# PSUM shared out anew in a four-layer graph kernel: three tiles for pairs, one for sums, one for rows

## The chip, the cores and the metric

The kernel runs on one core of a Trainium2 chip. A core has a matrix engine (TensorE, PE in the profile), a vector engine (VectorE, DVE), a scalar engine (ScalarE, ACT), a general engine (GpSimd, POOL) and a queue for DMA (SyncE, SP). Each engine works through its own queue of instructions in order and waits at semaphores for the others. The metric is the device time of one execution in microseconds (us), taken as the median of several runs. A profile shows one execution, with the start, the duration and the cause of waiting of every instruction.

## The reference

There are N = 4096 nodes with D = 64 features, and a dense 0/1 adjacency matrix `adj` of 4096x4096 float32 (64 MB). Four layers follow one another, each with a residual and a layer norm:

```python
x = _layernorm(x + _L0_gnn_ref(x, adj, L0_gnn_W, L0_gnn_b), axis=-1)
x = _layernorm(x + _L1_gnn_ref(x, adj, L1_gnn_r, L1_gnn_w_att, L1_gnn_b_att), axis=-1)
x = _layernorm(x + _L2_gnn_ref(x, adj, L2_gnn_weight, L2_gnn_bias), axis=-1)
x = _layernorm(x + _L3_gnn_ref(x, adj, L3_gnn_att_w, L3_gnn_att_b), axis=-1)
```

Layer 0 takes the mean over the neighbours, a linear map, a relu and a division by the norm. Layers 1 and 3 are hyperbolic attention: for every pair (i, j) of nodes the weight is `sigmoid(left_i + right_j) * adj_ij`, it multiplies the logarithmic map from x_i to x_j, and the sum over j is mapped back (`expmap`, `proj`). Layer 2 gives the last neighbours of each row the weights 1, 1/2, 1/4 and so on (by a count of the neighbours) and adds up a linear map of x with them.

## The kernel before, in words

The function `stream` (L569) computes everything on one core. Rows of the result are taken in 4 groups of 1024 (`GROUPS`, 3, 2, 1, 0). The nodes that are summed over come in 32 blocks of 128, taken in 16 pairs from the last to the first. Each layer reads `adj` once: a pair of blocks for one group is an edge tile of 128x2x1024 float32, 1 MB, loaded by SP's queue into a ring of six (`loads`). A program for inputs that don't fit this form stands behind it and isn't executed here.

**Attention** (`attention`, `attend`, `move`). For each block of a pair, six matmuls on PE put the pair values of 128 nodes with 1024 rows into a PSUM tile z of 128x1024 (L945, L948, L951, two halves of 512 each). ACT computes a sigmoid `sig` (L953) and a square `sq` of z (L956), DVE multiplies (L959, `t`). After both blocks DVE makes one more product over the pair (L961), and PE adds `t` up into the PSUM tile `acc` by four matmuls (L965). At the end of a group ACT copies `acc` to `sums` (L972). `move` (L982) then does the closing work of a group: some 75 small DVE operations on 128x8 (among them three reciprocal roots by Newton steps, L673 to L679), with the rows of `u_1` copied by ACT in two parts (L1002) out of a matmul (L1000), ACT's L1008 and L1034, POOL's L1007 and L1081, and DVE's L1085 as its end. `u_1` has one buffer. `linear` (L1088) prepares the next layer's supports, `prepare` (L791) and `spread_left` (L906) the rows and columns for the next attention.

**Layer 2.** For each block `count` (L1382) adds to a running count in a z tile by matmuls with two fixed matrices (`pass_by`, `enter`, L1386), ACT makes the weights by an exp (`weights_of`, L1395), and `add_up` (L1398, matmuls at L1401) multiplies them with the supports. `wide_pass` (L1323) treats groups 3 and 2 in turn within each block, two chains of counts; `narrow_pass` (L1353) then treats groups 1 and 0 one after another, by halves of 512 rows. `check` (L751) is a large DVE operation that tests the adjacency values, on one half of the edge tiles in layer 0 and the other half in layer 2.

**What sets the order.** Small work of the groups lies in two queues of generators; `tick(n)` lets them advance by n steps at fixed places of the main loops, `need` makes them run on until a part is done. In layers 0 and 2 the order of PE and ACT is that of the program text (`tc.manual_schedule` with `FIXED`); DVE's order there, and every engine's in layers 1 and 3, is set by the scheduler of the programming layer, from dependencies and its own estimates.

**PSUM.** There are eight banks of 128x512 float32. Before, z has two tiles of two banks, `acc` two of one bank, and `aux`, the tile for all small row work (`take`, `free`, `held`: the generators use it one after another), two of one bank.

Where group sums of layer 0 end, `end_0` (L1191) takes both `aux` tiles, one for each half of the group.

Of the kernel before, what the change touches and what calls it, by code (L numbers as in the profile page):

```python
# [10 lines left out]
F32 = mybir.dt.float32  # L11
# [10 lines left out]
D = 64  # L22
# [36 lines left out]
def gnn_stack_kernel(  # L59
# [509 lines left out]
    def stream(fits):  # L569

        with ExitStack() as st:
# [9 lines left out]
            aux = pool("f_aux", 2, space=PSUM)  # L581
# [323 lines left out]

            def spread_left(s):  # L906

                left_bs[s] = lefts.tile([P, WW], F32, name="left_b")
                for h in range(2):
                    yield from free()  # L910
                    t = take(F32, P, W)
                    for k in range(SB):
                        nb = s * WB + h * SB + k
                        nc.tensor.transpose(
                            t[:, k * P : (k + 1) * P],
                            left[:, nb : nb + 1].to_broadcast([P, P]),
                            ident,
                        )
                    yield near()
                    nc.scalar.copy(left_bs[s][:, h * W : (h + 1) * W], t)  # L920
                    held.pop()
                    yield 1

            def attend(layer, s, rate, then):
# [3 lines left out]
                acc = ps.tile([P, W], F32, name="acc")  # L928
                for g in reversed(range(NB // 2)):
# [4 lines left out]
                    sq = sb.tile([P, 2, WW], F32, name="sq")  # L934
                    t = sb.tile([P, 2, WW], F32, name="t")
                    for k in (1, 0):
# [3 lines left out]
                        zp = ps.tile([P, WW], F32, name="z")  # L940
                        for h in range(2):
                            half = zp[:, h * W : (h + 1) * W]
                            to = slice(s * WW + h * W, s * WW + (h + 1) * W)
                            at = k * WW + h * W
                            nc.tensor.matmul(  # L945
                                half, two_i, edge[:, at : at + W], start=True, stop=False
                            )
                            nc.tensor.matmul(  # L948
                                half, hi_lo[:, of], lo_hi[:, to], start=False, stop=False
                            )  # L950
                            nc.tensor.matmul(half, src[:, of], dst[:, to], start=False, stop=True)  # L951
                        sig = sb.tile([P, WW], F32, name="sig")
# [188 lines left out]
            with ExitStack() as lp:  # L1141
# [49 lines left out]
                def end_0(s, tops):  # L1191
                    z = grp("z0")
                    ts = []
                    yield from free()
                    for top, low in tops:
                        t = take(F32, P, SB, P)
                        for k in range(SB):
                            cols = slice(k * P, (k + 1) * P)
                            to = t[:, k, : D + 1]
                            nc.tensor.matmul(to, top[:, cols], sum_w, start=True, stop=False)  # L1200
                            nc.tensor.matmul(to, low[:, cols], count_w, start=False, stop=True)
                        ts.append(t)
                    for h, t in enumerate(ts):
# [74 lines left out]
            ps = pool("p_ps", 2, space=PSUM)  # L1278
# [44 lines left out]
            def wide_pass(two):  # L1323

                zs = [ps.tile([P, WW], F32, name="z") for _ in two]

                accs = [None, None]
                behind, lag = [None, None], []
                for g in reversed(range(NB // 2)):
                    edges = [load_2(s, g) for s in two]  # L1330
                    need((2, 2 * g // WB))
                    for k in (1, 0):
                        j = 2 * g + k
                        for i, edge in enumerate(edges):
# [15 lines left out]
                lag.pop(0)()  # L1350
                return accs

            def narrow_pass(s):  # L1353

                zs = [ps.tile([P, WW], F32, name="z") for _ in range(2)]
# [35 lines left out]
            def weights_of(z, n, w=None):  # L1391

                if w is None:
                    w = sb.tile([P, 2, WW], F32, name="sq").bitcast(BF16)[:, 0, :n]
                nc.scalar.activation(w, z[:, :n], AF.Exp, bias=at_edge, scale=-LN2)  # L1395
                return w
# [113 lines left out]
```

## Time and profile before

| quantity | before |
|---|---|
| median of 3 runs | 1141.41 us (1140.45 to 1144.33) |
| profiled execution, its own time | 1140.81 us |
| its span, first to last instruction | 1139.1 us |
| mean granted clock of PE | 0.972 |
| layer 0, until the first L959 | 0 to 190.8 us |
| layer 1, first L959 to the end of the last L961 | 190.8 to 532.3 us |
| layer 2, wide pass, then narrow passes | about 529 to 640, then to 775 us |
| layer 3, first L959 to the end of the last L961 | 775.7 to 1109.6 us |
| last L961 to the end | 29.5 us |

In the profile an engine's share is its busy time over the span. A line of the groups gives the operation, its output and inputs, its count, the busy time in us, the mean in ns, and the idle time just before it with what ended most of it. A line of the timeline gives the start, the duration, the instruction, and in brackets the idle time before it and its releaser. PEld is PE's loading of weights, which runs beside its matmuls. The stages overlap at their borders: the first counts of layer 2 start before the last product of layer 1 ends.

### The profile page before, as it was taken

The page shows a single profiled execution, that of the slowest core. Times are in us where ns is not written, and L with a number is a line of the kernel's source. Part 1 is how long each engine was busy: PE and PEld are TensorE (multiplying, and loading weights), DVE is VectorE, ACT ScalarE, POOL GpSimd, SP SyncE. Part 2 cuts the span into 40 slices and gives each one's busy share as a digit, 9 for nine tenths or more (in the row PEclk, how much of TensorE's full clock was granted, in tenths as well). Part 3 has the DMA queues.
Part 4 walks back from the last instruction along what each step waited for, and adds up shares of the span by engine and source line. Part 5 has one row for each costly group of instructions (what it writes and reads, how often), then busy time and mean ns, then how long its engine had stood idle before and what let it go on. Part 6 is the DMA issues. An engine that isn't in the chain of part 4 may idle for free.

```text
span 1139.1 us, 13626 instructions
## 1 busy us (share of the span) xinstructions
PE 1021.6 (90%) x4949; PEld 391.2 (34%) x4949; DVE 956.0 (84%) x1882; ACT 821.2 (72%) x894; POOL 66.1 (6%) x97
## 2 busy tenths in 40 slices
PE   6999897899999899998999997798899999998981
PEld 3545544233333333332333232232333333333320
DVE  6687898999999899999653476528999999999996
ACT  0003216899989789787766778888898998987970
POOL 0020120000000000100100020000000001001001
PEclk8999998999999999999999999899999999999995
DMA  8999998545666466564988976676455665665500
GB/s 342 422 391 405 373 415 337 196 166 203 215 206 219 154 209 221 180 204 154 322 305 301 341 263 233 233 257 231 164 206 188 218 222 194 222 221 183 196 0 23
DMA packets 38419, 271.58 MB, mean 238 GB/s; under 512 B 4550, under 2 KB 4550, under 8 KB 5574
## 3 DMA queue, kind: packets, MB, share of 16 engines
q1 hardware_dynamic: 37440, 269.50, 65.8%
q10 hardware_dynamic: 902, 1.12, 0.3%
q8 instruction: 41, 0.67, 0.2%
q14 instruction: 36, 0.29, 0.1%
HBM read 269.55 MB, written 1.05 MB: 238 GB/s over the span
## 4 chain that ended last, share of the span: by engine, by line
DVE 53%; PE 29%; ACT 8%; DMA 6%; POOL 2%; issue 2%; ACTq 0%; SPq 0%; POOLq 0%; DVEq 0%
DVE t L959 21%; DVE t L961 20%; PE z L1386 10%; DMA edges<-in_adj_dram 6%; PE acc L1401 5%; PE acc L1243 4%; PE acc L965 2%; ACT sig L953 2%; ACT sq L956 2%; ACT sq L1395 1%; PE aux L1106 1%; PE aux L852 1%; PE z L945 1%; DVE junk L751 1%; PE z L951 1%
## 5 line engine op out<-in xcount | busy, mean ns | idle before, releaser
L953 ACT ACTIVATE sig<-left_b,right 128x1024 f32<-128x1024 f32 x256 | 293.8, 1149 | 46.5 <-DVE t L959 36.5
L959 DVE SCALAR_TENSOR_TENSOR t<-z,sig 128x1024 f32<-128x1024 f32 x256 | 310.0, 1216 | 5.9 <-ACT sq L956 5.0
L956 ACT ACTIVATE sq<-z,turn 128x1024 f32<-128x1024 f32 x256 | 281.5, 1106 | 22.8 <-PE z L951 20.7
L961 DVE SCALAR_TENSOR_TENSOR t<-sq,t 128x2048 f32<-128x2048 f32 x128 | 292.9, 2288 | 0.7
L965 PE MATMUL acc<-t,xe 128*64 128x512 f32 x1024 | 255.2, 611 | 28.5 <-DVE t L961 24.4
L945 PE MATMUL z<-edges,two_i 128*128 128x512 bf16 x512 | 201.7, 394 | 21.5 <-DVE t L959 21.5
L951 PE MATMUL z<-dst,src 74*128 74x512 f16 x512 | 195.2, 381 | 0.0
L948 PE MATMUL z<-lo_hi,hi_lo 128*128 128x512 f16 x512 | 194.1, 379 | 0.0
L1395 ACT ACTIVATE sq<-z,at_edge 128x512 bf16<-128x512 f32 (+1 forms) x192 | 153.0, 830 | 53.3 <-PE z L1386 51.9
L965 PEld LDWEIGHTS acc<-t,xe 128*64 128x64 f32 x1024 | 63.6, 137 | 163.0 <-DVE t L961 85.9
L751 DVE SCALAR_TENSOR_TENSOR t<-edges 128x2048 bf16<-128x2048 f32 x32 | 74.0, 2312 | 44.2 <-DMA edges<-in_adj_dram 44.1
L1386 PE MATMUL z<-edges,pass_by 128*128 128x512 bf16 x248 | 89.6, 401 | 15.9 <-ACT sq L1395 15.8
L945 PEld LDWEIGHTS <-two_i 128*128 128x128 bf16 x512 | 50.2, 98 | 143.8 <-issue 96.6
L1243 PE MATMUL acc<-edges,first 128*128 128x512 bf16 x256 | 80.6, 396 | 20.0 <-DMA edges<-in_adj_dram 19.8
L1386 PE MATMUL z<-edges,enter 128*128 128x512 bf16 x256 | 90.8, 397 | 0.0
L1401 PE MATMUL acc<-sq,halves 128*64 128x512 bf16 x512 | 82.6, 401 | 3.6 <-ACT sq L1395 2.9
L1243 PE MATMUL acc<-edges,third 128*65 128x512 bf16 x256 | 80.5, 396 | 0.0
L751 DVE SCALAR_TENSOR_TENSOR junk<-edges 128x2048 bf16<-128x2048 f32 x32 | 73.1, 2285 | 4.7 <-DMA edges<-in_adj_dram 4.5
L948 PEld LDWEIGHTS <-hi_lo 128*128 128x128 f16 x512 | 50.3, 98 | 68.8 <-issue 25.5
L951 PEld LDWEIGHTS <-src 74*128 74x128 f16 x512 | 49.2, 96 | 67.5 <-issue 2.3
L1081 POOL TENSOR_TENSOR w_att<-x,p 128x512 f32<-128x512 f32 x8 | 12.9, 1615 | 495.0 <-DVE q L1079 495.0
L1243 PEld LDWEIGHTS <-first 128*128 128x128 bf16 x256 | 24.1, 98 | 48.9 <-issue 21.3
(262 smaller groups left out, 771.3 us busy)
## 6 DMA issues: line engine op xcount, KB each, us to landing
edges<-in_adj_dram SPq DMA_DIRECT2D x256, 1024.0 KB, 4.9
x<-in_x_dram SPq DMA_DIRECT2D x4, 256.0 KB
out_dram<-x ACTq DMA_DIRECT2D x4, 256.0 KB
w_sb<-in_L_gnn_W_dram ACTq DMA_DIRECT2D x1, 32.0 KB, 5.1
given<-in_L_gnn_b_dram ACTq DMA_DIRECT2D x1, 0.2 KB
given<-in_L_gnn_bias_dram ACTq DMA_DIRECT2D x1, 0.2 KB
given<-in_L_gnn_b_att_dram ACTq DMA_DIRECT2D x1, 0.0 KB
given<-in_L_gnn_att_b_dram ACTq DMA_DIRECT2D x1, 0.0 KB
```

Source lines behind the costliest of these rows:

```text
L751: V.scalar_tensor_tensor(junk, a, 0.0, a, ALU.not_equal, ALU.not_equal, accum_out=odd[:, n : n + 1])
L945: nc.tensor.matmul(half, two_i, edge[:, at : at + W], start=True, stop=False)
L948: nc.tensor.matmul(half, hi_lo[:, of], lo_hi[:, to], start=False, stop=False)
L951: nc.tensor.matmul(half, src[:, of], dst[:, to], start=False, stop=True)
L953: nc.scalar.activation(sig, left_b, AF.Sigmoid, bias=right[:, j : j + 1])
L956: nc.scalar.activation(sq[:, k], zp, AF.Square, bias=turn, scale=-1.0 / UNIT)
L959: V.scalar_tensor_tensor(t[:, k], zp, 0.0, sig, ALU.max, ALU.mult)
L961: V.scalar_tensor_tensor(t, sq, HIGH**2, t, ALU.add, ALU.mult)
L965: nc.tensor.matmul(acc[h * D : (h + 1) * D, :], xe[:, j, :], t[:, k, h * W : (h + 1) * W], start=j == BLOCKS[0], stop=j == BLOCKS[-1],)
L1243: nc.tensor.matmul(accs[h][:m], lhs[:, j, :], edge[:, at : at + W], start=j == BLOCKS[0], stop=j == BLOCKS[-1],)
L1386: nc.tensor.matmul(z[:, h : h + W], lhs, rhs[:, h : h + W], start=j == BLOCKS[0], stop=True, skip_group_check=True,)
L1395: nc.scalar.activation(w, z[:, :n], AF.Exp, bias=at_edge, scale=-LN2)
```

## The change

PSUM is shared out anew: z three tiles, `acc` one, `aux` one (3x2 + 1 + 1 banks). In attention the sums of a pair are issued two pairs later: after the z matmuls of the first block of pair g, those of pair g + 2 are added up, with an ordering edge (`in_order`) that keeps them behind these matmuls in the scheduler's order; the last two pairs of a group follow at its end. `sig` gets three buffers instead of two; `sq` and `t` are allocated after these matmuls. `end_0` takes its two halves one after another through the single `aux`. In the wide pass of layer 2, the counts of both chains stand side by side, then the sums of both, one block late: c c w w instead of c w c w. Both accumulators lie in one z tile, and one `sq` tile holds the weights of both chains. The narrow pass is only renamed.

```diff
-            aux = pool("f_aux", 2, space=PSUM)
+            aux = pool("f_aux", 1, space=PSUM)
...
+            def in_order(one, behind):
+
+                tc.add_manual_dep(
+                    one, behind.name,
+                    mybir.DependencyInfo(
+                        mybir.DependencyClass.NoSync, mybir.DependencyReason.DATA
+                    ),
+                    reason="order of issue",
+                )
...
+                lag = []
+
+                def add_up(g, t, behind=None):
+
+                    for k in (1, 0):
+                        j = 2 * g + k
+                        for h in range(2):
+                            it = nc.tensor.matmul(
+                                acc[h * D : (h + 1) * D, :], xe[:, j, :],
+                                t[:, k, h * W : (h + 1) * W],
+                                start=j == BLOCKS[0], stop=j == BLOCKS[-1],
+                            )
+                            if behind is not None:
+                                in_order(it.ins, behind.ins)
+
...
-                    sq = sb.tile([P, 2, WW], F32, name="sq")
-                    t = sb.tile([P, 2, WW], F32, name="t")
...
-                        zp = ps.tile([P, WW], F32, name="z")
+                        zp = z_tile()
...
+                        if k == 1:
+                            if len(lag) == 2:
+                                add_up(*lag.pop(0), last)
+                            sq = sb.tile([P, 2, WW], F32, name="sq")
+                            t = sb.tile([P, 2, WW], F32, name="t")
+                        sig = sb.tile([P, WW], F32, name="sig", bufs=3)
...
-                    for k in (1, 0):
-                        j = 2 * g + k
-                        for h in range(2):
-                            nc.tensor.matmul(
-                                acc[h * D : (h + 1) * D, :], xe[:, j, :],
-                                t[:, k, h * W : (h + 1) * W],
-                                start=j == BLOCKS[0], stop=j == BLOCKS[-1],
-                            )
+                    lag.append((g, t))
                     tick(rate)
+                for args in lag:
+                    add_up(*args)
...
-                    ts = []
-                    yield from free()
-                    for top, low in tops:
+                    for h, (top, low) in enumerate(tops):
+                        yield from free()
                         t = take(F32, P, SB, P)
...
-                        ts.append(t)
-                    for h, t in enumerate(ts):
...
                         V.tensor_mul(zz, t[:, :, :D], over(d))
+                        held.pop()
                         V.tensor_add(zz, zz, xw[:, at, :])
-                    held.clear()
+                        if h == 0:
+                            yield near()
...
-            ps = pool("p_ps", 2, space=PSUM)
+            ps = pool("p_ps", 1, space=PSUM)
+
+            def z_tile():
+                return ps.tile([P, WW], F32, name="z", bufs=3)
...
-                zs = [ps.tile([P, WW], F32, name="z") for _ in two]
-
-                accs = [None, None]
+                zs = [z_tile() for _ in two]
+
+                both = z_tile()
+                accs = [both[:, :W], both[:, W:]]
...
+                        w = sb.tile([P, 2, WW], F32, name="sq").bitcast(BF16)[:, :, :WW]
                         for i, edge in enumerate(edges):
                             here = edge[:, k * WW : (k + 1) * WW]
                             count(zs[i], behind[i], here, j, WW)
                             behind[i] = here
-                            while lag:
-                                lag.pop(0)()
-                            w = weights_of(zs[i], WW)
-
-                            def add(i=i, j=j, w=w):
-                                if accs[i] is None:
-                                    accs[i] = ps.tile([P, W], F32, name="acc")
-                                add_up(accs[i], j, w[:, :W], w[:, W:])
-
-                            lag.append(add)
+                            weights_of(zs[i], WW, w[:, i])
+                            if i == 1:
+                                for of, acc in enumerate(accs if lag else ()):
+                                    add_up(acc, *lag[of])
+                                lag = [(j, w[:, n, :W], w[:, n, W:]) for n in range(2)]
...
-                lag.pop(0)()
+                for of, acc in enumerate(accs):
+                    add_up(acc, *lag[of])
```

More of the change, by code (lines that the diff above doesn't have):

```diff
@@ L950, in attend @@
                             )
-                            nc.tensor.matmul(half, src[:, of], dst[:, to], start=False, stop=True)
-                        sig = sb.tile([P, WW], F32, name="sig")
+                            last = nc.tensor.matmul(
+                                half, src[:, of], dst[:, to], start=False, stop=True
+                            )
+                        if k == 1:
[4 more added lines that the diff above has]
+                        sig = sb.tile([P, WW], F32, name="sig", bufs=3)
                         nc.scalar.activation(
@@ L1337, in wide_pass @@
                             behind[i] = here
[L1338 to L1347 removed]
+                            weights_of(zs[i], WW, w[:, i])
[3 more added lines that the diff above has]
+                                lag = [(j, w[:, n, :W], w[:, n, W:]) for n in range(2)]
                             if two[0] != GROUPS[0] or j < BLOCKS[4]:
                                 tick(1)
[L1350 removed]
+                for of, acc in enumerate(accs):
+                    add_up(acc, *lag[of])
                 return accs
             def narrow_pass(s):
[L1355 removed]
+                zs = [z_tile() for _ in range(2)]
                 acc = ps.tile([P, W], F32, name="acc")
@@ L1389, in count, with weights_of @@
                             )
-            def weights_of(z, n, w=None):
-                if w is None:
-                    w = sb.tile([P, 2, WW], F32, name="sq").bitcast(BF16)[:, 0, :n]
+            def weights_of(z, n, w):
                 nc.scalar.activation(w, z[:, :n], AF.Exp, bias=at_edge, scale=-LN2)
-                return w
             def add_up(acc, j, *ws):
```

## The prediction

> **What bounds the kernel now.** I read the page's engine shares first, then the chain that ended last, then busy time by stage, and last the waits of the engine that leads the chain.
>
> ```profile
> PE 1021.6 (90%) x4949; PEld 391.2 (34%) x4949; DVE 956.0 (84%) x1882; ACT 821.2 (72%) x894; POOL 66.1 (6%) x97
> DVE 53%; PE 29%; ACT 8%; DMA 6%; POOL 2%; issue 2%; ACTq 0%; SPq 0%; POOLq 0%; DVEq 0%
> ```
> PE is busiest overall, but DVE carries the chain: PE's share is an average over stages with different limits. The stages are (us; busy of PE, PEld, DVE, ACT, POOL; granted clock; DMA share; GB/s):
>
> ```profile
> 280.00:361.00 81.00, 76.89 (x337) 26.84 (x336) 79.62 (x119) 72.55 (x71) 1.31 (x1) 1.00 0.61 208
> 534.00:639.00 105.00, 103.61 (x554) 34.22 (x551) 55.11 (x141) 72.94 (x75) 4.99 (x3) 1.00 0.84 298
> 702.00:775.00 73.00, 62.75 (x347) 20.55 (x347) 30.63 (x96) 63.10 (x94) 2.72 (x8) 0.91 0.69 237
> 1110.00:1139.00 29.00, 4.53 (x17) 1.53 (x13) 18.50 (x104) 2.08 (x5) 4.29 (x3) 0.56 0.07 22
> ```
> One group of attention (first row) has DVE busy 79.6 of 81: DVE-bound, PE close behind. The wide pass (second) is PE-bound, 103.6 of 105. The narrow pass (third) belongs to nobody: PE and ACT take turns, clock 0.91. The tail (fourth) is a chain of small DVE operations. Layer 0 (0 to 190) moves 391 GB/s at a DMA share of 0.97, and the change leaves its loads alone. What attention's DVE does, and what it waits for in layer 1 (190 to 535):
>
> ```profile
> L959 DVE SCALAR_TENSOR_TENSOR t<-z,sig 128x1024 f32<-128x1024 f32 x256 | 310.0, 1216 | 5.9 <-ACT sq L956 5.0
> L961 DVE SCALAR_TENSOR_TENSOR t<-sq,t 128x2048 f32<-128x2048 f32 x128 | 292.9, 2288 | 0.7
> DVE d L1013 <- POOL w_att L1007: 4.6, 2, 3.5
> DVE t L959 <- ACT sq L956: 3.0, 4, 1.9
> DVE uu L1011 <- ACT sq L1008: 1.5, 1, 1.5
> ```
> Waits for PSUM tiles hardly reach DVE. What DVE has besides these two are the small operations of `move`, and their spacing matters:
>
> ```profile
> 1109.75 0.17 DVE L678 SCALAR_TENSOR_TENSOR rs_t<-rs_t,mt 128x8 f32<-128x8 f32 x1
> 1109.95 0.17 DVE L679 SCALAR_TENSOR_TENSOR n<-rs_t,n 128x8 f32<-128x8 f32 x1
> 1110.51 0.16 DVE L1071 TENSOR_TENSOR p<-p,n 128x8 f32<-128x8 f32 x1
> 1110.58 0.16 DVE L1072 TENSOR_TENSOR q<-q,n 128x8 f32<-128x8 f32 x1
> ```
> Start to start: 0.20 us if the second needs the first's result, 0.08 if not. A lone one among the large ones is nearly free: from starts in attention, L959 to L961 takes 1.258 directly and 1.134 + 0.114 = 1.248 with a small one between; L959 to L959 takes 1.154 or 1.134 + 0.077.
>
> **What the Trainium skill says.** "VectorE: DVE Perf Modes", section The DRAIN you can't avoid: the next DVE operation doesn't start until the pipe has emptied; the 0.20 against 0.08 fits that. "ScalarE: Activation LUTs", section Table sets: the hidden batching unit: changing the function table costs a load of about 2.7 us; here one load shows 1.28. "TensorE: Matmul & The Clock Gate", section What's actually happening: an idle PE drops to half clock; here the granted clock falls to 0.5 for 3.4 to 6.8 us after idles of 2.5 us or more. "PSUM — Partial Sum Buffer", section The four PSUM rules: eight banks; before they are 2x2 + 2 + 2, after 3x2 + 1 + 1, so every tile gained is taken from another use. No run yet shows what one `aux` costs.
>
> **The change, part by part.** Besides the diff I use the order of each engine's instructions in the changed program. Instruction counts stay, but for one extra table pair.
>
> *Third z tile, sums two pairs late, third sig (layers 1 and 3).* Per pair, DVE takes 2x1.154 + 0.1 + 2.3 = 4.7 us, PE 12x0.222 + 1.9 = 4.6, ACT 4x1.13 = 4.5. So DVE stays the bound, and PE's freedom is worth only the waits. In layer 1, the spacings above, summed over its 128 L959, 64 L961, small operations and checks (L751, 2.29 us), give 328.7 us; from the first L959 (190.8) to the end of the last L961 (532.3) it took 341.5. The difference, 12.8, is waits and gaps; in layer 3 it is 333.9 - 325.0 = 8.9. With more slack I expect about 7 and 6: -5.8 and -2.9. Bounds: all gone -12.8 and -8.9; nothing 0; below nothing if the single `acc` or `aux` now blocks PE's queue.
>
> *The scheduler places small operations differently.* In the changed order they stand singly between large ones. Pairs in which one directly follows another that it needs fall from 30 to 1 in layer 1 and from 27 to 1 in layer 3. Each saves 0.20 - 0.05 = 0.15: 4.4 and 3.9. Some 40 more in each layer have not been issued by the last L961 (0.06 each among large ones, 2.4): -6.8 and -6.3. One check also leaves layer 1: -2.2. But these operations are put off, not removed (below).
>
> *Layer 0's end.* With one `aux`, the second half of `end_0` waits for the first to be read: the first L959 of layer 1 comes about 1.65 later. Layer 1 therefore ends at -6.8 - 2.2 - 5.8 + 1.65 = -13.1.
>
> *Boundary of layers 1 and 2.* In layer 2, PE and ACT orders are fixed by hand. ACT runs 12 exps, then the copy L1002 of the last group's `u_1`. That tile has one buffer, which the group before it frees with its L1085. Before:
>
> ```profile
> 544.70 0.69 DVE L1085 TENSOR_TENSOR x<-u,w_att 128x512 f32<-128x512 f32 x1 [0.93 <-POOL w_att L1081]
> 550.74 0.37 ACT L1002 COPY u<-aux 128x260 f32<-128x260 f32 x1
> ```
> L1085 was done 5 us early, 13.1 after the last L961. In the changed order six checks (13.7 us) and a longer rest of the chain (14.9, overlapping 0.5) precede it: 28.1 after the last L961, while ACT gets to L1002 about 15.4 after it. ACT stalls 12.6; behind L1002 queue the exps, behind those PE's counts: idle, then some 2.5 us at half clock. +15.1. Bounds: if ACT arrives as late as before (18.4) and only three checks come first, 28.1 - 6.9 - 18.4 = 2.8; if checks also wait for loads, about 20.
>
> *Wide pass.* PE: four counts and four sums take 1.559, two chains 3.118. Switches between the two kinds cost 0.091 + 0.074 more than going on in kind; side by side there is half as many: 2.966. Saved 0.152 x 30 = 4.6, and 0.9 where accumulators were renewed: -5.5. It is PE's own time in a PE-bound stage; a loss would need exps to come late, and an exp is 1.11 of 1.48 per chain.
>
> *Narrow pass.* The two sigs of layer 3's start fall in layer 2, as before:
>
> ```profile
> 703.19 1.28 ACT L953 ACT_TABLE_LOAD   x1
> 704.49 1.15 ACT L953 ACTIVATE sig<-left_b,right 128x1024 f32<-128x1024 f32 x1
> 705.65 1.28 ACT L1395 ACT_TABLE_LOAD   x1
> 707.69 0.59 PE L1386 MATMUL z<-edges,pass_by 128*128 128x512 bf16 x1 [2.71 <-ACT sq L1395]
> ```
> With three buffers, a third one is pulled in: 1.28 + 1.15 + 1.28 = 3.7 of ACT, PE idle some 2.7 as above, then half clock: +4.5 (bounds: 0, if hidden, to 6). The sig itself is then ready earlier in layer 3: -0.7.
>
> *Layer 3 and the tail.* -6.3 - 2.9 = -9.2 by the last L961. After it some 60 small operations of the group before remain, against 22 before; 38 x 0.17 = 6.5 later, and only then the last group's `move` gets `u_1`. The second half of the last copy waits for the single `aux`: +0.8. Tail +7.3; nothing covers it.
>
> *Sum.* -13.1 + 15.1 - 5.5 + 4.5 - 0.7 - 9.2 + 7.3 = -1.6. On the profiled execution (1140.81, a span of 1139.1 and 1.7 around it) that is 1139.2; the median of the runs, 1141.41, is 0.6 above that execution, so 1139.5.
>
> **Rivals.** *Near wash* (likeliest, 0.40): as summed, 1139.5; its own range 1133 to 1146. *The stall is small* (0.30): fewer checks come before L1085, or ACT is itself late, and attention loses most of its waits. Stall of 2.8 and half clock instead of 15.1: -9.8; waits -4 further: about 1125. For it: DVE was busy only 55 of 105 in the wide pass; against: ACT's order is fixed, and DVE's queue is in order too. *Slower, by one mechanism* (0.22): ACT's queue stands still at L1002 for 20 instead of 12.6, because checks ahead of L1085 wait for edge tiles which are freed only when PE, standing behind ACT, has used them. That adds 7.4, with half clock longer some 9: 1149. It decides from a stall of about 18 on (1139.5 + 5.4 = 1144.9). For it: DMA share 0.84 there, and a ring of six tiles; against: six tiles hold three pairs of both chains, ahead of PE. *No effect* (0.08): DVE sets attention, spacing gains are equalled by tails, and the waits stay: 1141 to 1145.
>
> **How the numbers follow.** No change is within 0.3%, 3.4 us, what a measurement of this kernel can tell: 1138.0 to 1144.8. Near wash gives faster 0.16, same 0.14, slower 0.10; small stall, faster 0.30; slower 0.22; no effect 0.06 same, 0.02 slower. Together 0.46, 0.20, 0.34. The range takes in most of small stall and most of slower: 1126 to 1151.
>
> **What would show it.** Right: the last L961 of layer 1 about 13 earlier than 532.3; ACT L1002 with an idle of some 12 released by DVE L1085, the clock at 0.5 after it; counts and sums at 2.97 per two-chain block; three table pairs in the narrow pass; layer 3 from first L959 to last L961 in about 325; last L961 to the end in about 37 rather than 29.5. Wrong: L1002 not waiting; PE or ACT waiting on `aux` or `acc` inside attention; or L959 waiting on sq more than the 3.0 of before.

## The result

The changed kernel takes 1150.66 us (median of 8 runs, 1144.69 to 1154.07) against 1141.72 for the kernel before on the same chip (8 runs). The ratio is 1.0069, with a 95% interval of 1.0052 to 1.0087: slower by 0.7%. A second comparison, in a later batch of runs (e14 below), gave 1.0055 (1.0032 to 1.0078). The forecast was 1139.5, faster by a hair, so its sign was wrong.

The page of the changed kernel, shares and chain:

```profile
PE 1024.2 (90%) x4949; PEld 402.2 (35%) x4949; DVE 952.8 (83%) x1882; ACT 809.8 (71%) x896; POOL 72.9 (6%) x97
PE 48%; DVE 35%; issue 6%; ACT 4%; DMA 3%; POOL 2%; SPq 0%; ACTq 0%; POOLq 0%; DVEq 0%
```
The busy times hardly differ from before, and the chain has gone over from DVE (53% to 35%) to PE (29% to 48%). Neither says where time was lost. The stages do. Lines of the changed kernel are later in its file: L989 and L991 are what L959 and L961 were, L946 the sums (L965), L1027 the copy of `u_1` (L1002), L1110 the end of `move` (L1085), L1418 the exp (L1395), L1224, L1230 and L1232 the end of layer 0 (L1200, L1208, L1209). Both profiled executions, us, with the borders read from the starts and ends of these lines ("first product" is L959 or L989, "pair product" is L961 or L991). The last column is the difference between a second pair of profiles, taken later on one chip (e13 and e14 below):

| stage | before | after | difference | forecast | second pair |
|---|---|---|---|---|---|
| start to first product of layer 1 | 190.8 | 198.3 | +7.5 | +1.65 | +9.8 |
| layer 1, to the end of the last pair product | 341.5 | 333.1 | -8.4 | -14.8 | -12.0 |
| layer 2, to the first product of layer 3 | 243.4 | 250.3 | +6.9 | +13.4 | +12.2 |
| layer 3, to the end of the last pair product | 333.9 | 325.1 | -8.8 | -9.2 | -7.5 |
| tail, to the end of the span | 29.5 | 37.3 | +7.8 | +7.3 | +7.7 |
| span | 1139.1 | 1144.1 | +5.0 | -1.6 | +10.1 |

A profile is one execution: the changed kernel's first one took 1145.96 us, among the fastest of its eight, so its +5.0 is less than the 8.9 between the medians.

From the first product on, the changed kernel is 2.5 us *faster* in the first pair, about as forecast (-3.3), and equal in the second. In sum the loss lies ahead of it, in layer 0 and its end, which the forecast had as an item of 1.65.

The two costliest groups of attention, and the changed kernel by stages (as before: us; busy of PE, PEld, DVE, ACT, POOL; clock; DMA share; GB/s):

```profile
L989 DVE SCALAR_TENSOR_TENSOR t<-z,sig 128x1024 f32<-128x1024 f32 x256 | 309.8, 1218 | 9.2 <-PE acc L946 6.7
L991 DVE SCALAR_TENSOR_TENSOR t<-sq,t 128x2048 f32<-128x2048 f32 x128 | 292.9, 2288 | 0.4
```

```profile
290.00:365.00 75.00, 73.46 (x322) 25.31 (x322) 74.66 (x105) 68.68 (x68) 1.20 (x1) 1.00 0.62 223
531.00:560.00 29.00, 16.57 (x91) 6.53 (x89) 25.34 (x89) 12.46 (x14) 1.56 (x1) 0.86 0.50 182
560.00:636.00 76.00, 74.98 (x416) 29.85 (x416) 38.61 (x103) 52.35 (x57) 2.21 (x2) 0.96 0.80 294
702.00:780.00 78.00, 65.50 (x369) 22.10 (x367) 30.29 (x91) 69.32 (x102) 2.74 (x8) 0.91 0.69 237
1107.00:1144.00 37.00, 6.41 (x17) 2.61 (x17) 24.30 (x145) 2.39 (x6) 4.30 (x3) 0.50 0.05 17
```
The large products take what they took. In a group of attention (first row) DVE is now all but gapless, 74.66 of 75. In the row of the border (second), PE is busy for only 16.6 of 29 us, and the clock is 0.86. The tail (last) has 145 DVE operations where the kernel before had 104.

**Layer 0.** What PE waits for between 40 and 182 us, in the kernel before and then in the changed one (waited for, us in total, times, longest):

```profile
PE acc L1243 <- DMA edges<-in_adj_dram: 10.9, 16, 1.4
```

```profile
PE aux L852 <- DVE z L1230: 3.2, 4, 0.8
PE acc L1267 <- DMA edges<-in_adj_dram: 2.7, 4, 1.3
PE aux L864 <- DVE xw L1214: 1.6, 1, 1.6
PE aux L1224 <- ACT top L1290: 1.6, 1, 1.6
PE aux L1224 <- DVE z L1230: 0.8, 1, 0.8
```
Before, PE waits for edge tiles alone: it is ahead of the loads. Afterwards it stands at `aux`, because the transposes of `prepare` and both halves of `end_0` share one tile and PE's order is fixed, and it has little lead left. In this execution the stream of layer 0 (its large matmuls, L1243 or L1267) still ends at 179.2, against 178.6 before, so nearly all of the 7.5 us comes after it. The second half of the last group suffers most. In the kernel before (DVE, then ACT's load of the sigmoid's table):

```profile
185.00 0.42 DVE L1209 TENSOR_TENSOR z<-z,xw 128x256 f32<-128x256 f32 x1
185.80 1.28 ACT L953 ACT_TABLE_LOAD   x1
```
In the changed kernel:

```profile
192.67 0.42 DVE L1232 TENSOR_TENSOR z<-z,xw 128x256 f32<-128x256 f32 x1
193.25 1.28 ACT L983 ACT_TABLE_LOAD   x1 [4.38 <-DVE z L1232]
```
The first sigmoid of layer 1 waits for the last reading of layer 0's `xw`. Both kernels have this order; before, L1209 was done 0.4 us before ACT came. Between the halves the transposes for `lo_hi` (at 186.8 on PE) took the single `aux`, and the second half's matmuls started at 190.1 in place of 182.4, behind two blocks of z.

**Border of layers 1 and 2.** As forecast, ACT stands before the copy of `u_1`, for 12.7 us:

```profile
545.10 1.11 ACT L1418 ACTIVATE sq<-z,at_edge 128x1024 bf16<-128x1024 f32 x1 [0.17 <-PE z L1411]
558.92 0.38 ACT L1027 COPY u<-aux 128x260 f32<-128x260 f32 x1 [12.71 <-DVE x L1110]
```
L1110 ends at 558.9, 27.5 after the last pair product (forecast 28.1); ACT was there at 546.2.

**Attention.** DVE's waits in layer 1 of the changed kernel (198 to 532):

```profile
DVE t L989 <- PE acc L946: 5.9, 6, 2.6
DVE lr L874 <- PE aux L864: 2.7, 1, 2.7
DVE d L1038 <- POOL w_att L1032: 2.2, 2, 1.7
```
The first line is new: `t` has two buffers, and a product now waits until the sums have read its buffer. That the sums are late is not the reason: with sums right behind their pair (e11 below) the same wait is 4.5 us.

### The profile page after: what moved, and what is told of

Same layout as the page of the kernel before. It is cut to its first block, busy times and chain, and to the rows that moved or that the text cites. A ratio compares the mean times of both kernels' runs of the same rounds, so it can differ in the third digit from the quotient of the medians.

```text
span 1144.1 us, 13889 instructions
## 1 busy us (share of the span) xinstructions
PE 1024.2 (90%) x4949; PEld 402.2 (35%) x4949; DVE 952.8 (83%) x1882; ACT 809.8 (71%) x896; POOL 72.9 (6%) x97
## 4 chain that ended last, share of the span: by engine, by line
PE 48%; DVE 35%; issue 6%; ACT 4%; DMA 3%; POOL 2%; SPq 0%; ACTq 0%; POOLq 0%; DVEq 0%
DVE t L989 11%; PE acc L946 11%; DVE t L991 9%; PE z L1411 8%; PE z L968 5%; PE acc L1267 5%; PE z L971 5%; PE z L974 5%; DMA edges<-in_adj_dram 3%; PE z L1423 2%; PE acc L1423 2%; ACT sq L1418 2%; DVE junk L751 2%; DVE t L751 1%; PE aux L852 1%
## 5 line engine op out<-in xcount | busy, mean ns | idle before, releaser
L989 DVE SCALAR_TENSOR_TENSOR t<-z,sig 128x1024 f32<-128x1024 f32 x256 | 309.8, 1218 | 9.2 <-PE acc L946 6.7
L983 ACT ACTIVATE sig<-left_b,right 128x1024 f32<-128x1024 f32 x256 | 292.2, 1147 | 10.2 <-DVE t L989 5.7
L991 DVE SCALAR_TENSOR_TENSOR t<-sq,t 128x2048 f32<-128x2048 f32 x128 | 292.9, 2288 | 0.4
L946 PE MATMUL acc<-t,xe 128*64 128x512 f32 x1024 | 261.0, 613 | 21.3 <-DVE t L991 17.6
L1418 ACT ACTIVATE sq<-z,at_edge 128x512 bf16<-128x512 f32 (+1 forms) x192 | 150.3, 828 | 47.7 <-PE z L1411 45.3
L946 PEld LDWEIGHTS acc<-t,xe 128*64 128x64 f32 x1024 | 64.3, 137 | 151.5 <-issue 79.0
L1267 PE MATMUL acc<-edges,first 128*128 128x512 bf16 x256 | 82.1, 403 | 10.2 <-DMA edges<-in_adj_dram 10.0
L1267 PE MATMUL acc<-edges,third 128*65 128x512 bf16 x256 | 82.1, 403 | 0.0
L971 PEld LDWEIGHTS <-hi_lo 128*128 128x128 f16 x512 | 50.4, 98 | 56.0 <-issue 11.7
L1125 ACT COPY x_t<-aux 64x512 f32<-64x512 f32 x16 | 9.2, 573 | 51.0 <-PE aux L1120 51.0
L1423 PE MATMUL acc<-sq,halves 128*64 128x512 bf16 x256 | 41.8, 403 | 0.2 <-ACT sq L1418 0.2
```

The costliest lines, as they stand in the source:

```text
L946: it = nc.tensor.matmul(acc[h * D : (h + 1) * D, :], xe[:, j, :], t[:, k, h * W : (h + 1) * W], start=j == BLOCKS[0], stop=j == BLOCKS[-1],)
L971: nc.tensor.matmul(half, hi_lo[:, of], lo_hi[:, to], start=False, stop=False)
L983: nc.scalar.activation(sig, left_b, AF.Sigmoid, bias=right[:, j : j + 1])
L989: V.scalar_tensor_tensor(t[:, k], zp, 0.0, sig, ALU.max, ALU.mult)
L991: V.scalar_tensor_tensor(t, sq, HIGH**2, t, ALU.add, ALU.mult)
L1267: nc.tensor.matmul(accs[h][:m], lhs[:, j, :], edge[:, at : at + W], start=j == BLOCKS[0], stop=j == BLOCKS[-1],)
```

## The experiments

My theory after the result was that the time goes three ways: the single `aux` at layer 0, the copy of `u_1` at the border, and small operations put off into the tail; and that the third z tile brings attention's gain. The rival was that putting the sums off makes the loss. Ratios below are to the kernel before on the same chip, with their 95% interval. Stage times are from each kernel's own profile, one execution each: e1 to e4 ran on one chip, e5 to e8 on a second, e9 to e12 on a third, e13 to e15 on a fourth. Where a tail is given here, it runs from the last pair product to the end of the last L1110 (L1085), 24.9 in the kernel before and 32.7 in the changed one. A "small" DVE operation is one of less than 0.8 us; in a "held pair" two small ones follow each other and the second starts only when the first has ended (at most 0.06 us later), as where it needs the first's result.

### One part alone or undone

**`u_1` in two buffers (e1)**, in the changed kernel:

```diff
-                all_u = row.tile([P, WB, D + 1], F32, name="u_1")
+                all_u = row.tile([P, WB, D + 1], F32, name="u_1", bufs=2)
```

> The changed kernel with two buffers for u_1, so that the copy of the last group's rows need not wait for the group before. Theory (the stall at this copy is ACT's and PE's own loss): the idle of 12.7 us before the copy goes, and the half clock after it: about 12 us less than the changed kernel, near 1138 against its 1150.7. Rival (DVE is late at this border anyway, and what waits there is only moved): less than 4 us faster than the changed kernel, and a wait of similar length behind DVE somewhere else in the wide pass.

Measured 1140.77, ratio 0.9978 (0.9961 to 0.9996), against 1.0069 for the changed kernel: 9.9 us less by the medians. The stall is gone from ACT's timeline:

```profile
546.64 0.37 ACT L1027 COPY u<-aux 128x260 f32<-128x260 f32 x1
```
Layer 2 falls from 250.3 to 243.7, and the tail by 3.1, since there too the last group had waited for `u_1` (ACT for 8.6 us at L1027). One word of code turns the change from slower into slightly faster. But of a stall of 12.7 only 6.6 comes back in layer 2, and the rival is right for the rest: part of the wait has moved. What PE waits for in this stage (531 to 640), in the changed kernel and then in this one:

```profile
PE aux L1025 <- ACT u L1027: 12.3, 1, 12.3
```

```profile
PE aux L1120 <- DVE halves L1142: 3.5, 1, 3.5
PE aux L1120 <- DVE x L1110: 3.3, 1, 3.3
```
PE now stands twice at the single `aux`, for 6.8 us in all, before transposes that follow the closing work; from 560 to 580 its clock is 0.85. The theory holds by about half in layer 2.

**Late sums alone (e2)**: `attend` with its `lag` list and `in_order`, all else as before.

```diff
-                        zp = z_tile()
+                        zp = ps.tile([P, WW], F32, name="z")
-                        sig = sb.tile([P, WW], F32, name="sig", bufs=3)
+                        sig = sb.tile([P, WW], F32, name="sig")
```
(against the changed `attend`; pools and the wide pass as in the kernel before)

> The kernel before with the sums of a pair two pairs late and nothing else: z two tiles, acc two, aux two, sig two. Theory (the losses come from sharing out PSUM anew, by the single aux and by the scheduler's other order): layer 1 begins at 190.8 as before, no stall at the border, time between 1136 and 1144. Rival (putting the sums off is what delays: t is held longer, DVE waits for it): L959 waits on the sums by 10 us or more in layers 1 and 3, and 1148 or more.

Measured 1188.05, ratio 1.0396 (1.0344 to 1.0447). My theory of harmless late sums falls: layer 1 takes 360.1 and layer 3 359.1. The time is the rival's, but DVE hardly waits on the sums, as the rival had it (layer 1, 192 to 552):

```profile
DVE t L989 <- ACT sq L986: 16.6, 35, 1.8
DVE d L1038 <- POOL w_att L1032: 1.8, 3, 1.2
```
It waits 35 times for a square, thus for z. The likely cause, which no run tests alone: with two z tiles, the sums (1.9 us of PE) between a pair's two z's stand in the way just when a tile comes free. A second part is order: 72 and 79 held pairs in layers 1 and 3, in the kernel before 29 and 29. Late sums cost time with two z tiles (here) and none that can be measured with three (e10 and e11 below).

**PSUM's new split alone (e3)**: three z, one `acc`, one `aux`, with the old `attend` and the old order of the wide pass. Against the changed kernel's `attend`:

```diff
-                for args in lag:
-                    add_up(*args)
+                    for k in (1, 0):
+                        j = 2 * g + k
...
```

> PSUM shared out as in the changed kernel (three z, one acc, one aux, halves of layer 0's end one after another), but sums right behind their pair, two sigs and the wide pass's old order of counts and sums. Theory (PSUM's split makes the losses): layer 1 starts some 5 to 8 us late, layers 1 and 3 shorter by about 8 each, the tail longer by about 7, time 1148 to 1156. Rival (the late sums make the losses): within 3 us of the kernel before.

Measured 1158.85, ratio 1.0141 (1.009 to 1.0191). Layers 1 and 3 take 332.8 and 328.7, layer 2 256.6, the tail as in the changed kernel, first product at 195.5. The time lies above the 1148 to 1156 of the theory, but the theory holds in kind: the split makes both attention's gain and the losses. The gain is DVE's order: held pairs fall from 29 and 29 in the kernel before to 5 and 4 here (1 and 1 in the changed kernel).

**The wide pass's order alone (e4)**, in the kernel before:

```diff
-                            while lag:
-                                lag.pop(0)()
-                            w = weights_of(zs[i], WW)
...
+                            weights_of(zs[i], WW, w[:, i])
+                            if i == 1:
+                                for of, acc in enumerate(accs if lag else ()):
+                                    add_up(acc, *lag[of])
```

> The kernel before with the wide pass's order alone: counts of both chains, then sums of both, in the two acc tiles. Theory (PE sets the wide pass, fewer switches between the two kinds of matmul): a two-chain block takes 2.97 us in place of 3.12, the kernel 4 to 6 us less, near 1137. Rival (the loads or ACT's exps come to set the pass): less than 2 us.

Measured 1140.17, ratio 0.9974 (0.9958 to 0.999). In its profile layer 2 takes 236.4 in place of 243.4, all else as before (341.6 and 334.0). The profile shows more than the theory's 4 to 6, the medians less (2.8). That it is faster is clear, by how much only to a few us.

**One `aux` alone (e5)**, in the kernel before:

```diff
-            aux = pool("f_aux", 2, space=PSUM)
+            aux = pool("f_aux", 1, space=PSUM)
```
(with the changed `end_0`)

> The kernel before with one aux tile instead of two (and the halves of layer 0's end one after another, as that needs), all else as before: z two, acc two. Its instruction order leaves 57 small DVE operations and three checks between the last L961 of layer 1 and the end of the group before; before has 26 and three, the changed kernel 75 and six. Theory (the single aux makes the losses at layer 0's end and part of those at the border and in the tail): first L959 some 5 us late, layer 1 no shorter, tail about 4 us longer, time 1147 to 1154. Rival (the losses belong to the third z tile, by which the scheduler always finds a large operation ready): within 3 us of the kernel before.

Measured 1158.82, ratio 1.0131 (1.0091 to 1.017). First product at 200.9, layer 1 349.8, the tail 4.9 longer. The theory holds for layer 0 and the tail, and layer 1 is worse than I thought: DVE stands idle there for 21.0 us in place of 10.0, counting stretches above 0.06. The whole is longer than the theory's 1147 to 1154. Layer 3 is 5.5 *shorter* without any third tile: fewer of the closing operations fall there (267 small ones in place of 289), probably because that work is held up at `aux`.

**Layer 0's end uninterrupted (e6)**, in the changed kernel:

```diff
+                    yield from free()
                     for h, (top, low) in enumerate(tops):
-                        yield from free()
...
-                        if h == 0:
-                            yield near()
```

> The changed kernel, but nothing else may take the aux tile between the two halves of layer 0's end. Theory (first L959 of layer 1 comes 7.5 us late because transposes of the group before get the single aux between the halves): first L959 at 191 to 194 in place of 198.3, and 4 to 6 us less than the changed kernel. Rival (layer 1 starts late for the half clock or the loads, whatever takes aux): first L959 still at 196 or later, less than 2 us.

Measured 1152.93, ratio 1.0083 (1.0059 to 1.0108): no gain, as the rival had it. The fair comparison is with the next run, e7, which leaves the end of layer 0 as it was in the changed kernel and ran on the same chip. The end itself is shorter: from the last matmul of layer 0's stream to the first product 14.2 in place of 17.5. But the stream ends later, at 191.1 in place of 186.8, and the first product comes at 205.3 in place of 204.4. PE now waits within its fixed order for the first half to be read (2.5 us in three waits, in e7 0.8 in one). So the interruption isn't the whole loss; where one tile has two users, the wait was moved and not removed.

**Two sigs (e7)**, in the changed kernel:

```diff
-                        sig = sb.tile([P, WW], F32, name="sig", bufs=3)
+                        sig = sb.tile([P, WW], F32, name="sig")
```

> The changed kernel with two sig buffers. Theory: the third sigmoid is no longer pulled into layer 2's narrow pass, two pairs of table loads in place of three there, PE's idle of 2.2 us at 725 goes: 2 to 5 us less from the last exp of the wide pass to the first L959 of layer 3, and the first sigmoid of layer 1 need not wait for a tile of layer 0 that L1232 still reads. Rival (PE and ACT make good for it within the pass): less than 1.5 us.

Measured 1152.77, ratio 1.008 (1.0054 to 1.0106). The third pair of table loads is gone, but from the last exp of the wide pass to the first product of layer 3 that is worth 1.3 (137.8 to 136.5), and layers 1 and 3 are 2.3 and 1.5 longer. One pair of executions can't tell 1.3 from scatter, but all profiles together agree: this stretch is 137.6 on average in the eight kernels' profiles with two sigs (135.7 to 139.5) and 139.1 in the nine with three (137.8 to 140.7). The rival holds. The first sigmoid still waits for L1232, so that wait is not the third buffer's doing.

**All three together (e8)** (`u_1`, the uninterrupted end, two sigs):

> The changed kernel with u_1 in two buffers, layer 0's end uninterrupted and two sigs. Theory (the three losses are separate and add): 10 + 5 + 3 less than the changed kernel, 1131 to 1135, faster than the kernel before by about 9. Rival (they hide each other, since the late start of layer 1 and the border's stall both let loads and checks run ahead): 1138 or more.

Measured 1146.18, ratio 1.0022 (1.0007 to 1.0038). The rival's number, not its reason: the rest of the kernel is about as in the run with two `u_1` alone (layer 2 245.0, tail 29.4), and on this chip it is 6.6 to 6.8 below e7 and e6, which had one `u_1`. But the first product comes at 208.9, 10.1 later than in e1. Part of that goes with the chip or the execution, since e7 has it at 204.4 without the uninterrupted end. Layer 0 of this kernel (us, busy times, then clock, DMA share, GB/s):

```profile
40.00:180.00 140.00, 126.84 (x662) 72.14 (x661) 101.71 (x278) 24.70 (x41) 19.10 (x23) 0.89 0.91 358
```
The changed kernel has 0.98, 0.97 and 390 there. The loads, which bound layer 0 before, wait for PE.

### What the losses amount to

**A second `aux` tile in layer 0 alone (e9)**, where a bank is free (the changed kernel; the tiles are used in turn):

```diff
-                return aux.tile(list(shape), dtype, name="aux")
+                of = (aux, *more)[len(turns) % (1 + len(more))]
+                turns.append(1)
+                return of.tile(list(shape), dtype, name="aux")
...
+                more.append(lp.enter_context(tc.tile_pool(name="m0_aux", bufs=1, space=PSUM)))
...
+            more.clear()
             place[0] = 1
```

> The changed kernel with a second aux tile during layer 0 alone (a bank is free there), used in turn with the first. Theory (with one aux tile, PE's fixed order in layer 0 stands still at transposes and at layer 0's end, falls to half clock after each, and lags behind the loads by a different amount in every execution): the half clock in the first 210 us falls from 14 to 22 us lost to about 7, first L959 at 191 to 194 in place of 198 to 205, the median 6 to 10 below the changed kernel, about 1142, and the scatter of some 10 us narrows to about 4. Rival (the late start comes from the chip or the loads and not from aux): median within 3 us of the changed kernel and the same scatter.

Measured 1146.79 (1142.62 to 1154.3, 20 runs), ratio 1.0039 (1.0021 to 1.0056). About 4 below the changed kernel's first median, and 8.5 us of clock lost in the first 210 us (each stretch counted by what was withheld) in place of 13.7, first product at 194.2. So the tile seems to matter, by half of what the theory had at most: against the changed kernel's second comparison (1.0055, 1.0032 to 1.0078) the gain is not clear of the noise. The scatter did not narrow; that part of the theory falls. The last group's end runs after the second tile is given up and still takes 17.5 from the last stream matmul to the first product; the kernel before takes 12.2.

**And `u_1` in two buffers (e10):**

> As the run before, and u_1 in two buffers. Theory (the two losses are in different stages and add): 10 us less than the run before, 1130 to 1134, faster than the kernel before by 0.7 to 1.0%. Rival (they overlap): less than 5 us below the run before.

Measured 1137.77, ratio 0.9959 (0.9934 to 0.9984): 9.0 less than the run before: two `u_1` are worth the same here as in e1, so that loss is separate from layer 0's. The level of the theory, 1130 to 1134, is missed because the run before missed its own, and what the second `aux` adds to e1 (0.9978, 0.9961 to 0.9996) is within the noise.

**And the sums right behind their pair (e11):**

> As the run before, with the sums of a pair right behind it. Theory (the third z tile brings attention's gain, late sums matter little beside it): layers 1 and 3 within 4 us each of 333 and 325, the time 0 to 5 us more. Rival (the late sums bring the gain): layers 1 and 3 at about 341 and 334, 12 us more or above.

Measured 1137.54, ratio 0.9951 (0.9934 to 0.9968). Layers 1 and 3 take 331.5 and 326.5. With three z tiles the late sums change nothing that can be measured. It has the lowest median here, 0.5% below the kernel before and clear of it.

**In e10, DVE tied to the program text in layer 3's last group (e12):**

```diff
-                        V.scalar_tensor_tensor(t[:, k], zp, 0.0, sig, ALU.max, ALU.mult)
+                        it = V.scalar_tensor_tensor(t[:, k], zp, 0.0, sig, ALU.max, ALU.mult)
+                        if layer == 3 and s == GROUPS[-1]:
+                            tc.keep_in_program_order(it)
```

> As e10, with DVE's order in layer 3's last group tied to the program text, by which the closing work of the group before is done before the last L961. Theory (small operations put off are only moved): the tail 7 us shorter, 29.6 to about 22, and layer 3 longer by about 9, as 86 more of them follow another directly: within 3 us of e10. Rival (in the attention they fill waits): layer 3 longer by less than 4, 4 us or more below e10.

Measured 1147.5, ratio 1.004 (1.002 to 1.006), 9.7 above e10. The tail is 5.4 shorter (24.2), layer 3 17.2 longer. Both theories missed: the work is not merely moved. DVE's idle stretches above 0.06 us in layer 3 hardly differ (7.4, in e10 6.1), so it isn't waiting; it is busy for 13.2 longer. 58 more small operations than in e10 lie in layer 3, and there are 67 held pairs in place of 2. By the prices of the prediction, 58 x 0.06 + 65 x 0.15 = 13.2, which is that difference.

**Both kernels on one chip (e13, e14), and layer 0's last end in a z tile (e15).** What was open was whether the late first product belongs to the single `aux` or to chip and execution.

> The kernel before once more, for a profile on the chip of the next two runs. Theory (single aux makes the late start): first L959 at 190 to 193, half clock costing at most 8.5 us of clock in the first 210 us. Rival (chip and execution make it): first L959 at 196 or later here too, or as late as in the next run.

Measured 1142.9, ratio 1.0005 (0.999 to 1.0019); first product at 190.3, 6.8 us of clock lost.

> The changed kernel once more on that chip. Theory: first L959 6 us or more behind the run before, 13 us or more of clock lost in the first 210 us, and from the first L959 on 940 to 942 us to the last operation, as in its first profile. Rival: first L959 within 3 us of the run before, and the difference later.

Measured 1149.82, ratio 1.0055 (1.0032 to 1.0078). First product at 200.1, 9.8 behind the run before. From there to the last operation 943.2 against 942.7: the rest of the two kernels is equal within 0.5. Of the 9.8, the stream's end takes 4.3 (182.5 for 178.2), what follows it the other 5.4. The theory holds, but for the clock: 10.2 lost, not 13 or more. Half clock is a part of the delay, not its measure.

```diff
-                        t = take(F32, P, SB, P)
+                        t = take(F32, P, SB, P) if big is None else big[:, h]
```
(e15 against e11: `big` is a z tile for both halves of the last group)

> As e11 (u_1 in two buffers, second aux tile during layer 0, no late sums), and the last group's end of layer 0, which runs when that second tile is gone, puts both halves into a z tile instead of aux. Theory: first L959 at 191 to 193 in place of 194.8, the rest as e11: about 1135, 0.6 to 0.9% below the kernel before. Rival: first L959 at 194 or later, no faster than e11.

Measured 1140.72, ratio 0.9976 (0.9962 to 0.9991), first product at 196.5, no faster than e11. The rival holds. In this kernel ACT's copy `src` waits for its transposes until 190.3, and the first sigmoid comes behind it: with the halves out of the way, `prepare` queues at `aux` instead.

First product and end of layer 0's stream, over all profiles (us):

| `aux` tiles | stream's last matmul | first product |
|---|---|---|
| two (before, e13, e2, e4) | 178.2 to 179.9 | 190.3 to 192.0 |
| two in layer 0, then one (e9 to e12, e15) | 176.7 to 181.5 | 194.2 to 197.4 |
| one (after, e14, e1, e3, e5 to e8) | 179.2 to 194.7 | 195.5 to 208.9 |

The first row stands clear of the other two. That one tile makes layer 0's end late is shown on two chips: 200.1 against 190.3 (e14, e13), and 195.5 and 198.8 (e3, e1) against 192.0 and 191.7 (e2, e4). The smallest edit, e5, has it at 200.9, but no kernel with two tiles was profiled on its chip. Why the amount changes so much among kernels with one tile is not settled. The four latest (200.9 to 208.9, e5 to e8) come from one chip, and only one execution of each kernel was profiled.

## Why the prediction was wrong

**What failed: the step "Layer 0's end", +1.65.** I costed only the wait of the second half for the first, on an idle PE. The runs showed +7.5 and, in the second pair of profiles, +9.8. The step missed three things. Other users (the transposes of `prepare`) get the tile between the halves; what stands behind on PE's fixed order, the stream itself, can be held up too (by 0.6 in the first pair, 4.3 in the second); and a first sigmoid that was covered by 0.4 us is the next to be late, by 4.4. I also read layer 0 as safe because "the change leaves its loads alone": a stage bound by its loads stays so only while PE keeps its lead of 10.9 us of waits, and PE's share of 165 in 190 us left little room.

**Luck in the sum.** With this step put right, the sum would have come to about +4, near the +5.0 of the first pair. But there layer 1 missed by +6.4 and layer 2 by -6.5, and the two cancelled. In the second pair both lie within 3 of the forecast. Single executions of one kernel differ by some 3 us in these stages (layer 1 of the kernel before: 341.5 and 344.5), so the first pair alone can't judge these terms.

**Right: the stall at L1002.** Forecast 12.6, measured 12.71. The net of border and wide pass was +9.6 by forecast; from the last pair product of layer 1 to the wide pass's last exp it was +7.5 (105.0 to 112.5), with the wide pass's order worth 7.0 (e4) for a forecast of 5.5. What the forecast didn't see is that the single `aux` stands right behind this stall, so that removing it gives only 6.6 in layer 2 (e1).

**Right: small operations in attention.** Forecast -6.8 - 2.2 = -9.0 in layer 1 and -6.3 in layer 3; DVE's busy time fell by 9.9 (332.4 to 322.5) and by 7.0 (325.9 to 318.9), in the second pair by 10.2 and 7.1, and held pairs fell from 29 and 29 to 1 and 1.

**Not borne out: fewer waits in attention.** I had them fall by 5.8 and 2.9. DVE's idle stretches above 0.06 us add up to 10.0 before and 12.3 after in layer 1, and 12.8 and 11.7 in the second pair; in layer 3, 6.8 and 6.0, then 5.4 and 6.0. There is no clear fall. The waits of L989 for a square (3.0 before) are nearly gone, but waits for the sums, 5.9, have come in their place. So the small operations (and the check that leaves layer 1) make attention's gain alone.

**Right: the tail.** +7.8 for +7.3. In e12, forcing the closing work in between cost more in layer 3 (17.2) than it saved in the tail (5.4).

**Wrong in size: the third table pair.** I took +4.5; e7 puts it at 1.3. It is there, with PE's idle of 2.2 behind it (ACT, then PE, of the changed kernel):

```profile
720.91 1.28 ACT L983 ACT_TABLE_LOAD   x1
722.21 1.15 ACT L983 ACTIVATE sig<-left_b,right 128x1024 f32<-128x1024 f32 x1
723.37 1.28 ACT L1418 ACT_TABLE_LOAD   x1
725.41 0.58 PE L1411 MATMUL z<-edges,pass_by 128*128 128x512 bf16 x1 [2.18 <-ACT sq L1418]
```
Over all profiles the difference between two and three sigs is 1.5.

**The rivals.** "Slower, by one mechanism" came out on the right side at 1149, by the wrong mechanism: the stall was 12.7, not 20. That the single `aux` might block PE's queue stood in my text as a bound within attention, and was never costed where PE's order is fixed.

**The half clock.** The Trainium skill, "TensorE: Matmul & The Clock Gate", section What's actually happening, puts half clock after at least one idle window of about 3.4 us. I had applied it to the border and the narrow pass only, with idles of 2.5 us or more. Layer 0 shows half clock too (e8, 0.89 on average from 40 to 180 us), and after waits much shorter than that figure, as the last section lists; even the kernel before has it at 21.2 us, after a wait of 1.5. Here the measurement decides. And of the rule that a DVE operation doesn't start until the pipe has emptied, only the dependent operations (0.20) are an instance: the independent operations (0.08) start while the one before, 0.16 long, still runs.

## What to carry to other kernels

A buffer that is taken from a shared pool must be priced at every place that shares it, with what is queued behind it on an engine whose order is fixed; here PSUM banks moved from small work to large made two layers 17 us shorter, and the time was lost again at three places: the end of layer 0, the border of layers 1 and 2, and the tail, to which small work was put off. A wait that a profile shows as zero may be covered by tenths of a microsecond: ask for each wait how much cover it has. And after such a change, look first for a buffer that became too few: two for `u_1` were worth 9.9 and 9.0 us (e1, e10). Then look what stands behind it: when that stall went, PE waited 6.8 us for the next single tile.

## What the runs showed of the hardware

In layer 0 of the changed kernel, stretches of half clock (at 56.8, 155.8 and 183.1) followed PE waits of only 0.83, 1.61 and 1.59 us, counting waits within 3.4 us of their start. Waits of that size don't always bring it: one of 1.32 at 90.1 was followed by none. The first 210 us of the changed kernel have five stretches (27 us in all, 13.7 lost), those of the kernel before two (13.6 us, 6.8 lost). And dependent small DVE operations, drawn back to back between the large ones, cost in e12 what the spacings of the kernel before say: 13.2 us more of DVE's busy time for 58 more operations and 65 more held pairs, an estimate from those spacings of 13.2. My estimate of 9 for the layer fell short of them.
